# Selective state-space layer on one core: how B and C reach the partitions, how many decay tiles there are, and how the states are summed

## The chip, the cores and the metric

The kernel runs on 1 core of one Trainium2 chip. The metric is device time in microseconds (us), median of the runs. Engines are named as in the profile: PE is TensorE (matmuls; PEld its weight loads), DVE is VectorE, ACT is ScalarE, POOL is GpSimd, SP is SyncE, which here only issues DMAs. SBUF is the working memory of 128 partitions, PSUM a smaller memory of 8 banks per partition (a bank holds 512 float32 columns), into which PE writes.

## The reference

Four layers follow each other on x of shape (16, 256, 256): 16 sequences of T = 256 steps and 256 features. Layer 0 is a low-rank adapter, layer 1 a block with two selective state-space models (one over the sequence, one over the sequence reversed) and an MLP, layers 2 and 3 are attention blocks with MLPs. All is float32. The part that matters here is the state-space model of layer 1, with 512 inner channels and 64 states for each:

```python
xz = h @ in_w
xs, z = jnp.split(xz, 2, axis=-1)
xs = jax.nn.silu(xs)
proj = xs @ xproj_w
dt = jax.nn.softplus(proj[..., :D_INNER] + dt_bias)
Bm = proj[..., D_INNER:D_INNER + D_STATE]
Cm = proj[..., D_INNER + D_STATE:]
A = -jnp.exp(A_log)

def step(hst, ins):
    dt_t, B_t, C_t, x_t = ins
    dA = jnp.exp(dt_t[:, :, None] * A)
    hst = hst * dA + (dt_t * x_t)[:, :, None] * B_t[:, None, :]
    y_t = jnp.einsum('bds,bs->bd', hst, C_t)
    return (hst, y_t)
_, ys = jax.lax.scan(step, h0, (tm(dt), tm(Bm), tm(Cm), tm(xs)))
y = jnp.swapaxes(ys, 0, 1) + xs * Dskip
return y * jax.nn.silu(z) @ out_w
...
h_fwd = _ssm(h, fwd_in_w, ...)
h_bwd = jnp.flip(_ssm(jnp.flip(h, 1), bwd_in_w, ...), 1)
x = x + gate * (h_fwd + h_bwd)
```

## The kernel before

Channels lie on partitions, time on columns. The 512 inner channels are IC = 4 chunks of 128, so a tile of all channels of one sequence is 128 x 4 x 256, or 128x1024. A unit is one sequence in one direction; there are 32. Each unit has NS = 64 states, so the main loop (lines 1145 to 1180) takes 2048 steps k, one state s of one unit u each. For a state:

- `drive` (913), called four steps ahead (AHEAD = 4): POOL multiplies dt*x by this state's row of B and makes h (line 931). The row of B is on all partitions in `bb`, which SP loads for four states at a time by a DMA that reads a row of DRAM once for every partition (`load_b`, 898).
- `decay` (935), called one step ahead: ACT makes exp(dt * A), one instruction a chunk of 128 channels (line 946), into PSUM. The tile holds two chunks, one bank; there are ND = 3 such tiles, used in turn, so a state takes two of them. Column 0 of each chunk is set to 0 once (line 270) and never written again: it ends one chunk's recurrence before the next begins.
- `scan` (965): DVE runs the recurrence over 512 columns at a time, two instructions a state, in place in h (line 974). For the reversed direction the scan reads and writes its columns backwards. Then h is multiplied by the state's row of C. For five states in eight ("near": s % 8 in 0, 2, 3, 5, 6) DVE does it (977), with C in the PSUM tile `cs`, to which PE copies it with two transposes (`spread`, 955); for the other three ("far") POOL does it (981), with C in `cb`, which a DMA loads for the three of eight states (`load_c`, 904).
- `add_up` (984), called two steps later (BEHIND = 2): PE adds h to y in PSUM (line 992), with h as the stationary operand, in eight transposes of 128x128. y therefore has time on partitions. At a unit's end it is copied to SBUF (1165), transposed back (1172) and multiplied with the gate z (1173).

Beside the loop, a few instructions a step, run generators: `beside` (the end of the last unit, `back`, and the projections of the next but one, `front`) and `other` (`rest`: the MLP of layer 1 and layers 2 and 3 of a sequence that is through the state-space part). They share ACT, DVE and PE with the loop; attention adds reductions to DVE (577, 682) and exponentials and copies to ACT. After the last unit the rest of the last sequence runs alone, with the loop's PSUM banks (`alone`).

The order of the instructions on each engine is fixed when the program is built: a scheduler arranges them by what it holds to be ready, and at run time each engine takes them strictly in that order. Only the instructions under `keep_in_program_order` (most of POOL's) stay as written. Between engines, semaphores carry the dependencies: a decay tile is written again only when its last reader on DVE is done, an h buffer (tag h, NH = 11 of them) only when PE has added it.

Of the kernel before, what the change touches and what calls it, by code (L numbers as in the profile page):

```python
# [15 lines left out]
P = 128  # L16
# [5 lines left out]
IC = DI // P  # L22
NS = 64
EPS = 1e-5


COLUMNS = [
# [27 lines left out]
def kernel(ctx: ExitStack, tc: tile.TileContext, a: dict, out: bass.AP):  # L55
# [66 lines left out]


    SG = 4
    ND = 3
    NH = 11
    res = ctx.enter_context(tc.tile_pool(name="res", bufs=1))
    xp = ctx.enter_context(tc.tile_pool(name="xp", bufs=3))
    ws = ctx.enter_context(tc.tile_pool(name="ws", bufs=2))
# [5 lines left out]
    ps_c = ctx.enter_context(tc.tile_pool(name="ps_c", bufs=1, space=PSUM))  # L135
    ps_g = ctx.enter_context(tc.tile_pool(name="ps_g", bufs=2, space=PSUM))

    def chunked(w):
# [234 lines left out]
    def front(u):  # L373
# [27 lines left out]
        yield  # L401
# [5 lines left out]
        bd = bdram.tile([P, T], F32, name="bd")  # L407
        nc.sync.dma_start(bd, bc)
        yield
        pt = bank1("pct")  # L410
        for t in range(NT):
            nc.tensor.transpose(pt[:, t * P : (t + 1) * P], bc[:, t * P : (t + 1) * P], ident)
        cT = s2.tile([P, NT, NS], F32, name="cT")
        nc.scalar.copy(cT, pt[:, :T].rearrange("p (t s) -> p t s", t=NT)[:, :, NS:])
        yield


        pr = s1.tile([P, IC, T], F32, name="pr")
        for m in range(0, IC, 2):
# [42 lines left out]
        st[u] = (xz, cT, bd, dt, dtx)  # L462
        yield

    def back(u, yg):

        b, d = units[u]
        st.pop(u)
        yield
        po = halves(bank1("po"))  # L470
        for m in range(DC):
            for c in range(IC):
                nc.tensor.matmul(
                    po[:, m], w_out[d][:, c, m * P : (m + 1) * P], yg[:, c],
                    start=(c == 0), stop=(c == IC - 1),
                )
            yield
        for m in range(DC):
            xb = xs[b][:, m]
            nc.vector.scalar_tensor_tensor(  # L480
                xb, po[:, m], m_mamba[:, 4 + m, b : b + 1], xb, ALU.mult, ALU.add
            )
        if d == 1:
            waiting.append(rest(b))
        yield
# [404 lines left out]
            yield from front(following)  # L890


    bbs, cbs, ys, made, hs, skips = {}, {}, {}, {}, {}, {}
    cs = ps_c.tile([P, 2, T], F32, name="cs")
    steps = [(u, s) for u in range(len(units)) for s in range(NS)]
    turn = [0]

    def load_b(u, g):
        bd = st[u][2]
        bb = s3.tile([P, SG, T], F32, name="bb")  # L900
        nc.sync.dma_start(bb, bd[g * SG : (g + 1) * SG, :].partition_broadcast(P))
        bbs[u, g] = bb

    def load_c(u, g):
        bd = st[u][2]
        cb = s3.tile([P, 3, T], F32, name="cb")
        nc.sync.dma_start(
            cb,
            bd[NS + 8 * g + 1 : NS + 8 * g + 8 : 3, :].partition_broadcast(P),
        )  # L910
        cbs[u, g] = cb

    def drive(k):
        u, s = steps[k]
        if s % SG == 0:
            if s == 0:
                load_b(u, 0)
            if s + SG < NS:
                load_b(u, s // SG + 1)
            if s % 8 == 0:  # L920
                load_c(u, s // 8)
# [6 lines left out]
        h = s3.tile([P, IC, T], F32, name="h", bufs=NH)  # L928
        bb = bbs[u, s // SG][:, s % SG]
        tc.keep_in_program_order(  # L930
            nc.gpsimd.tensor_tensor(h, st[u][4], bb.unsqueeze(1).to_broadcast([P, IC, T]), ALU.mult)  # L931
        )
        hs[k] = h

    def decay(k):
        u, s = steps[k]
        d = units[u][1]

        when = slice(1, T) if d == 0 else slice(T - 2, None, -1)
        made[k] = []  # L940
        for i in range(2):
            dc = decays[turn[0] % ND]
            turn[0] += 1
            for j in range(2):
                c = 2 * i + (j if d == 0 else 1 - j)
                nc.scalar.activation(  # L946
                    dc[:, j, 1:T], st[u][3][:, c, when], AF.Exp, scale=a_neg[d][:, c, s : s + 1]
                )
            made[k].append(dc)


    near = [k for k, (u, s) in enumerate(steps) if s % 8 in (0, 2, 3, 5, 6)]
    nth = {k: i for i, k in enumerate(near)}

    def spread(i):

        if i >= len(near):
            return
        u, s = steps[near[i]]
        for t in range(NT):  # L960
            nc.tensor.transpose(  # L961
                cs[:, i % 2, t * P : (t + 1) * P], st[u][1][:, t, s : s + 1].to_broadcast([P, P]), ident
            )

    def scan(k):
        u, s = steps[k]
        d = units[u][1]
        h = hs[k]
        for i, dc in enumerate(made.pop(k)):
            hv = h[:, 2 * i : 2 * i + 2].rearrange("p c t -> p (c t)")  # L970
            dv = dc.rearrange("p c t -> p (c t)")
            if d == 1:
                hv = hv[:, ::-1]
            nc.vector.tensor_tensor_scan(hv, dv, hv, 0.0, ALU.mult, ALU.add)  # L974
        if k in nth:
            c = cs[:, nth[k] % 2]
            nc.vector.tensor_tensor(h, h, c.unsqueeze(1).to_broadcast([P, IC, T]), ALU.mult)  # L977
        else:
            c = cbs[u, s // 8][:, (s % 8) // 3]
            tc.keep_in_program_order(  # L980
                nc.gpsimd.tensor_tensor(h, h, c.unsqueeze(1).to_broadcast([P, IC, T]), ALU.mult)  # L981
            )

    def add_up(k):
        u, s = steps[k]
        if s == 0:
            ys[u] = ps_y.tile([P, NT, DI], F32, name="y")

        for n, h in enumerate(([skips.pop(u)] if s == 0 else []) + [hs.pop(k)]):
            for t in range(NT):  # L990
                for c in range(IC):
                    nc.tensor.matmul(  # L992
                        ys[u][:, t, c * P : (c + 1) * P], h[:, c, t * P : (t + 1) * P], ident,
                        start=(s == 0 and n == 0 and c == 0),
                        stop=(s == NS - 1 and c == IC - 1), is_transpose=True,
                        skip_group_check=True,
                    )

# [140 lines left out]
    for k in range(AHEAD):  # L1139
        drive(k)  # L1140
    decay(0)
    spread(0)
    spread(1)
    other = late()
    for k in range(len(steps) + BEHIND):
        if k < len(steps):
# [7 lines left out]
                decay(k + 1)  # L1154
        if k >= BEHIND:
            add_up(k - BEHIND)
        if k - 1 in nth:
            spread(nth[k - 1] + 2)
        if k >= BEHIND:
            u, s = steps[k - BEHIND]  # L1160
            if s == NS - 1:
                b, d = units[u]
                yt = s1.tile([P, NT, DI], F32, name="yt", tag="uu")
                for t in range(NT):
                    nc.scalar.copy(yt[:, t], ys[u][:, t])
                yg = s1.tile([P, IC, T], F32, name="yg", tag="pr")
                for i in range(2):
                    py = halves(bank1("py"))
                    for j in range(2):
                        c = 2 * i + j  # L1170
                        for t in range(NT):
                            nc.tensor.transpose(py[:, j, t * P : (t + 1) * P], yt[:, t, c * P : (c + 1) * P], ident)
                    nc.vector.tensor_tensor(
                        yg[:, 2 * i : 2 * i + 2], py, st[u][0][:, IC + 2 * i : IC + 2 * i + 2], ALU.mult
                    )
                pend = beside((u, yg), u + 2)
        step(pend)
        for _ in range(2 if k % 2 else 1):
# [1 line left out]
                other = waiting.pop(0) if waiting else None  # L1180
    drain(pend)
    drain(other)
    alone += [None] + [t.rearrange("p c t -> p (c t)") for t in (decays[0], cs, decays[1])]
    alone += [None, decays[2].rearrange("p c t -> p (c t)")]
    while waiting:
        drain(waiting.pop(0))

# [27 lines left out]
```

## Time and profile before

The three runs took 7622.63 us (median; 7620.03 to 7626.16).

| | |
|---|---|
| span of the profiled execution | 7616.3 us |
| first scan to last scan | 151 us to 7396 us |
| ACT, 8192 decays (line 946) | 1824.6 + 1816.8 us busy |
| POOL, 2048 products with B (931) | 4793.5 us busy |
| POOL, 768 products with C (981) | 1813.2 us busy |
| PE, 16384 sums (992) | 2385.3 us busy |
| PE, 2560 copies of C (961) | 521.6 us busy |
| DMA, share of 16 engines | 26.7% |

Busy time of an engine is the time in which at least one of its instructions ran. A group's line gives, after the bar, busy time, mean nanoseconds of one instruction, then the engine's idle time just before the group's instructions and what ended most of it. PE's instructions are pipelined, so the mean of one is more than the distance between two. The table of waits gives who waited for whom: total us, how often, the longest.

### The profile page before, as it was taken

The numbers are of one execution on the slowest core, as the hardware profiler recorded it, in microseconds if no ns is written. First come the engines' busy times: TensorE is split into PE (matmuls) and PEld (weight loads), VectorE is DVE, ScalarE is ACT, GpSimd is POOL, SyncE is SP. The second block draws the span as 40 slices with busy tenths as digits, with TensorE's granted clock in tenths as the row PEclk, the third lists the DMA queues.
The fourth block names the chain that finished last, engine by engine and source line by source line (L and its number), as shares of the span: only waits on it lengthen the run. The fifth ranks groups of instructions, "written<-read, shape, count | busy, mean of one in ns | idle before, by whom it ended". The sixth has DMA issues, their size and how long they took to land.

```text
span 7616.3 us, 100847 instructions
## 1 busy us (share of the span) xinstructions
PE 6249.2 (82%) x35471; PEld 4952.4 (65%) x35471; DVE 6860.6 (90%) x6887; ACT 5431.2 (71%) x12141; POOL 6843.8 (90%) x2959
## 2 busy tenths in 40 slices
PE   7568888888888888888888888888888888888778
PEld 4456676666667666676666666666666766666655
DVE  3988999999999999999999999999999999999982
ACT  4567777777777777777777777777777777777753
POOL 3999999999999999999999999999999999999960
PEclk8679999999999999999999999999999999999999
DMA  4112232222322222232222223222232222322221
GB/s 166 54 65 92 89 102 76 87 92 88 103 85 93 80 91 95 92 103 73 88 92 91 100 86 98 78 92 93 87 106 79 94 84 89 101 91 89 73 68 49
DMA packets 331644, 675.90 MB, mean 89 GB/s; under 512 B 24724, under 2 KB 204032, under 8 KB 326784
## 3 DMA queue, kind: packets, MB, share of 16 engines
q1 hardware_dynamic: 331136, 669.44, 26.7%
q8 instruction: 280, 4.59, 0.2%
q14 instruction: 228, 1.87, 0.1%
HBM read 650.22 MB, written 10.75 MB: 87 GB/s over the span
## 4 chain that ended last, share of the span: by engine, by line
DVE 47%; POOL 15%; issue 14%; ACT 12%; PE 10%; DVEq 0%; POOLq 0%; ACTq 0%
DVE h L974 34%; POOL h L931 8%; DVE h L977 8%; ACT decay L946 5%; POOL h L981 5%; PE y L992 3%; DVE maxima L682 1%; ACT L155 1%; PE dense L500 1%; PE down L511 1%; PE bank L108 1%; PE po L605 1%; POOL uu L452 1%; POOL dt L458 1%; POOL dtx L461 1%
## 5 line engine op out<-in xcount | busy, mean ns | idle before, releaser
L974 DVE TENSOR_TENSOR_SCAN h<-decay,h 128x512 f32<-128x512 f32 x4096 | 4748.8, 1213 | 283.1 <-ACT decay L946 196.6
L931 POOL TENSOR_TENSOR h<-dtx,bb 128x1024 f32<-128x1024 f32 x2048 | 4793.5, 2367 | 129.2 <-PE y L992 128.4
L992 PE MATMUL y<-ident,h 128*128 128x128 f32 x16384 | 2385.3, 292 | 693.0 <-POOL h L981 639.1
L992 PEld LDWEIGHTS y<-ident,h 128*128 128x128 f32 x16384 | 2054.6, 151 | 1047.6 <-POOL h L981 733.1
L946 ACT ACTIVATE decay<-dt,a_neg_bwd 128x255 f32<-128x255 f32 x4096 | 1816.8, 471 | 759.9 <-DVE h L974 718.3
L946 ACT ACTIVATE decay<-dt,a_neg_fwd 128x255 f32<-128x255 f32 x4096 | 1824.6, 474 | 613.0 <-DVE h L974 571.6
L981 POOL TENSOR_TENSOR h<-h,cb 128x1024 f32<-128x1024 f32 x768 | 1813.2, 2361 | 289.8 <-DVE h L974 275.1
L977 DVE TENSOR_TENSOR h<-h,cs 128x1024 f32<-128x1024 f32 x1280 | 1533.5, 1215 | 66.2 <-PE cs L961 56.6
L961 PE MATMUL cs<-ident,cT 128*128 128x128 f32 x2560 | 521.6, 294 | 131.8 <-DVE h L977 130.3
L961 PEld LDWEIGHTS cs<-ident,cT 128*128 128x128 f32 x2560 | 331.4, 147 | 216.0 <-DVE h L977 192.0
L572 PE MATMUL sc<-k,q 64*128 64x256 f32 x960 | 293.4, 429 | 16.7 <-ACT ex L581 16.0
L393 PE MATMUL pxz<-hTm,w_in 128*128 128x256 f32 x1024 | 267.6, 388 | 15.9 <-DVE maxima L682 12.1
L679 PE MATMUL sc<-kd,qk 128*128 128x512 f32 x490 | 251.4, 614 | 33.5 <-DVE maxima L682 20.8
L700 PE MATMUL scT<-qk,kd 128*128 128x256 f32 x984 | 251.1, 386 | 28.7 <-DVE qk L691 23.2
L581 ACT ACTIVATE ex<-sc,nmax 128x256 f32<-128x256 f32 x480 | 222.7, 468 | 71.2 <-DVE nmax L577 68.5
L423 PE MATMUL pdt<-xz,w_dt 128*128 128x256 f32 x1024 | 247.3, 385 | 0.0
L572 PEld LDWEIGHTS sc<-k,q 64*128 64x128 f32 x960 | 172.6, 200 | 105.3 <-issue 34.2
L393 PEld LDWEIGHTS pxz<-hTm,w_in 128*128 128x128 f32 x1024 | 181.4, 194 | 53.1 <-DVE maxima L682 15.5
L700 PEld LDWEIGHTS scT<-qk,kd 128*128 128x128 f32 x984 | 175.5, 190 | 60.7 <-ACT pr L429 25.0
L577 DVE TENSOR_REDUCE nmax<-sc 128x2 f32<-128x512 f32 x240 | 163.9, 683 | 49.5 <-PE sc L572 48.8
L423 PEld LDWEIGHTS pdt<-xz,w_dt 128*128 128x128 f32 x1024 | 190.7, 194 | 22.2
L595 ACT COPY exT<-pt 128x512 f32<-128x512 f32 x240 | 140.0, 583 | 86.2 <-PE pt L591 84.0
(350 smaller groups left out, 7571.4 us busy)
## 6 DMA issues: line engine op xcount, KB each, us to landing
bb<-bd SPq DMA_DIRECT2D x512, 512.0 KB
cb<-bd SPq DMA_DIRECT2D x256, 384.0 KB
l2w<-in_L_cond_W_dram SPq DMA_DIRECT2D x32, 1024.0 KB
l3w<-in_L_cond_W_dram SPq DMA_DIRECT2D x32, 1024.0 KB
l1w<-in_L_cond_mlp_w_dram SPq DMA_DIRECT2D x48, 512.0 KB
w_in<-in_L_cond_fwd_in_w_dram SPq DMA_DIRECT2D x16, 1024.0 KB
w_dt<-_L_cond_fwd_xproj_w_dram SPq DMA_DIRECT2D x16, 1024.0 KB
w_in<-in_L_cond_bwd_in_w_dram SPq DMA_DIRECT2D x16, 1024.0 KB
```

What stands on the lines that cost most here:

```text
L393: nc.tensor.matmul(px[:, j], w_in[:, c, (m + j) * P : (m + j + 1) * P], hT[:, c], start=(c == 0), stop=(c == DC - 1),)
L423: nc.tensor.matmul(pp[:, j], w_dt[:, c, (m + j) * P : (m + j + 1) * P], xz[:, c], start=(c == 0), stop=(c == IC - 1),)
L572: nc.tensor.matmul(sc[:, t], q[base : base + 64, ch, t * P : (t + 1) * P], k[base : base + 64, ch], start=True, stop=True,)
L679: nc.tensor.matmul(sc, q[:, g, t * P : (t + 1) * P], kd[g % 2][:, 2 * i : 2 * i + 2], start=True, stop=True)
L700: nc.tensor.matmul(sc[:, kt], kd[g % 2][:, j, kt * P : (kt + 1) * P], q[:, g], start=True, stop=True)
L931: nc.gpsimd.tensor_tensor(h, st[u][4], bb.unsqueeze(1).to_broadcast([P, IC, T]), ALU.mult)
L946: nc.scalar.activation(dc[:, j, 1:T], st[u][3][:, c, when], AF.Exp, scale=a_neg[d][:, c, s : s + 1])
L961: nc.tensor.transpose(cs[:, i % 2, t * P : (t + 1) * P], st[u][1][:, t, s : s + 1].to_broadcast([P, P]), ident)
L974: nc.vector.tensor_tensor_scan(hv, dv, hv, 0.0, ALU.mult, ALU.add)
L977: nc.vector.tensor_tensor(h, h, c.unsqueeze(1).to_broadcast([P, IC, T]), ALU.mult)
L981: nc.gpsimd.tensor_tensor(h, h, c.unsqueeze(1).to_broadcast([P, IC, T]), ALU.mult)
L992: nc.tensor.matmul(ys[u][:, t, c * P : (c + 1) * P], h[:, c, t * P : (t + 1) * P], ident, start=(s == 0 and n == 0 and c == 0), stop=(s == ...
```

## The change

- C: every state's row of C now comes by DMA, four states at a time (`load_c` is like `load_b`); the PE copies, the tile `cs` and the transposed `cT` go. Both kinds of state read C from `cb`.
- Decays: ND = 2 tiles, each of two PSUM banks, 1024 columns, a whole state. Column 0 of a chunk is no longer fixed: dt's column 0 is set to 1e34 (`APART`) by POOL once dt*x has been made, and A is kept at or below -1e-30 (`LEAST`), so the decay there is exp(-1e4 or less) = 0.
- Scan: one instruction of 1024 columns a state. For near states it writes into the decay tile in PSUM, and the multiply by C reads that tile and writes h; for far states it writes h as before.
- Reversed direction: the columns are turned once, when xz is copied out of PSUM, and turned back when `back` reads `po`; the scans run forward for both.
- Sums: PE keeps the identity as the stationary operand and h moves, two matmuls of 512 columns a state. y then has channels on partitions, and the end of a unit is one product with z.
- NH goes from 11 to 10; the list `alone` holds the four halves of the two decay tiles.

```diff
-    ND = 3
-    NH = 11
+    ND = 2
+    NH = 10
...
-        nc.vector.tensor_scalar(an, an, -1.0, None, ALU.mult)
+        nc.vector.tensor_scalar(an, an, -1.0, LEAST, ALU.mult, ALU.min)
...
-    decays = [ps_y.tile([P, 2, T], F32, name=f"decay{j}") for j in range(ND)]
-    for dc in decays:
-        nc.vector.memset(dc[:, :, 0:1], 0.0)
+    decays = [ps_y.tile([P, IC, T], F32, name=f"decay{j}") for j in range(ND)]
...
-            nc.scalar.copy(xz[:, m : m + 2], px)
+            nc.scalar.copy(xz[:, m : m + 2], px[:, :, ::-1] if d else px)
...
+        tc.keep_in_program_order(nc.gpsimd.memset(dt[:, :, 0:1], APART))
...
-                xb, po[:, m], m_mamba[:, 4 + m, b : b + 1], xb, ALU.mult, ALU.add
+                xb, po[:, m, ::-1] if d else po[:, m], m_mamba[:, 4 + m, b : b + 1], xb, ALU.mult, ALU.add
...
     def load_c(u, g):
-        bd = st[u][2]
-        cb = s3.tile([P, 3, T], F32, name="cb")
-        nc.sync.dma_start(
-            cb,
-            bd[NS + 8 * g + 1 : NS + 8 * g + 8 : 3, :].partition_broadcast(P),
-        )
+        bd = st[u][1]
+        cb = s3.tile([P, SG, T], F32, name="cb")
+        nc.sync.dma_start(cb, bd[NS + g * SG : NS + (g + 1) * SG, :].partition_broadcast(P))
...
-        when = slice(1, T) if d == 0 else slice(T - 2, None, -1)
-        made[k] = []
-        for i in range(2):
-            dc = decays[turn[0] % ND]
-            turn[0] += 1
-            for j in range(2):
-                c = 2 * i + (j if d == 0 else 1 - j)
-                nc.scalar.activation(
-                    dc[:, j, 1:T], st[u][3][:, c, when], AF.Exp, scale=a_neg[d][:, c, s : s + 1]
-                )
-            made[k].append(dc)
+        dc = decays[k % ND]
+        for c in range(IC):
+            nc.scalar.activation(dc[:, c], st[u][2][:, c], AF.Exp, scale=a_neg[d][:, c, s : s + 1])
...
     def scan(k):
...
-            nc.vector.tensor_tensor_scan(hv, dv, hv, 0.0, ALU.mult, ALU.add)
-        if k in nth:
-            c = cs[:, nth[k] % 2]
-            nc.vector.tensor_tensor(h, h, c.unsqueeze(1).to_broadcast([P, IC, T]), ALU.mult)
+        h, dc = hs[k], decays[k % ND]
+        c = cbs[u, s // SG][:, s % SG].unsqueeze(1).to_broadcast([P, IC, T])
+        if s % 8 in (0, 2, 3, 5, 6):
+            nc.vector.tensor_tensor_scan(flat(dc), flat(dc), flat(h), 0.0, ALU.mult, ALU.add)
+            nc.vector.tensor_tensor(h, dc, c, ALU.mult)
         else:
...
+            nc.vector.tensor_tensor_scan(flat(h), flat(dc), flat(h), 0.0, ALU.mult, ALU.add)
+            tc.keep_in_program_order(nc.gpsimd.tensor_tensor(h, h, c, ALU.mult))
...
     def add_up(k):
...
-            for t in range(NT):
-                for c in range(IC):
-                    nc.tensor.matmul(
-                        ys[u][:, t, c * P : (c + 1) * P], h[:, c, t * P : (t + 1) * P], ident,
-                        start=(s == 0 and n == 0 and c == 0),
-                        stop=(s == NS - 1 and c == IC - 1), is_transpose=True,
-                        skip_group_check=True,
-                    )
+            for i in range(0, IC, 2):
+                nc.tensor.matmul(
+                    ys[u][:, i : i + 2], ident, h[:, i : i + 2],
+                    start=(s == 0 and n == 0), stop=(s == NS - 1),
+                )
...
-                yt = s1.tile([P, NT, DI], F32, name="yt", tag="uu")
-                for t in range(NT):
-                    nc.scalar.copy(yt[:, t], ys[u][:, t])
                 yg = s1.tile([P, IC, T], F32, name="yg", tag="pr")
-                for i in range(2):
-                    py = halves(bank1("py"))
...
+                nc.vector.tensor_tensor(yg, ys[u], st[u][0][:, IC:], ALU.mult)
```

More of the change, by code (lines that the diff above doesn't have):

```diff
@@ L24 @@
 EPS = 1e-5
+APART, LEAST = 1e34, -1e-30
 COLUMNS = [
@@ L134 @@
     ps_y = ctx.enter_context(tc.tile_pool(name="ps_y", bufs=1, space=PSUM))
-    ps_c = ctx.enter_context(tc.tile_pool(name="ps_c", bufs=1, space=PSUM))
     ps_g = ctx.enter_context(tc.tile_pool(name="ps_g", bufs=2, space=PSUM))
@@ L408, in front @@
         nc.sync.dma_start(bd, bc)
-        yield
-        pt = bank1("pct")
-        for t in range(NT):
-            nc.tensor.transpose(pt[:, t * P : (t + 1) * P], bc[:, t * P : (t + 1) * P], ident)
-        cT = s2.tile([P, NT, NS], F32, name="cT")
-        nc.scalar.copy(cT, pt[:, :T].rearrange("p (t s) -> p t s", t=NT)[:, :, NS:])
         yield
@@ L461, in front @@
         tc.keep_in_program_order(nc.gpsimd.tensor_tensor(dtx, dt, xz[:, 0:IC], ALU.mult))
-        st[u] = (xz, cT, bd, dt, dtx)
+        tc.keep_in_program_order(nc.gpsimd.memset(dt[:, :, 0:1], APART))
+        st[u] = (xz, bd, dt, dtx)
         yield
@@ L890, in beside @@
             yield from front(following)
-    bbs, cbs, ys, made, hs, skips = {}, {}, {}, {}, {}, {}
-    cs = ps_c.tile([P, 2, T], F32, name="cs")
+    bbs, cbs, ys, hs, skips = {}, {}, {}, {}, {}
     steps = [(u, s) for u in range(len(units)) for s in range(NS)]
-    turn = [0]
     def load_b(u, g):
-        bd = st[u][2]
+        bd = st[u][1]
         bb = s3.tile([P, SG, T], F32, name="bb")
@@ L904, in load_c @@
     def load_c(u, g):
-        bd = st[u][2]
-        cb = s3.tile([P, 3, T], F32, name="cb")
-        nc.sync.dma_start(
-            cb,
-            bd[NS + 8 * g + 1 : NS + 8 * g + 8 : 3, :].partition_broadcast(P),
-        )
+        bd = st[u][1]
+        cb = s3.tile([P, SG, T], F32, name="cb")
+        nc.sync.dma_start(cb, bd[NS + g * SG : NS + (g + 1) * SG, :].partition_broadcast(P))
         cbs[u, g] = cb
@@ L919, in drive @@
                 load_b(u, s // SG + 1)
-            if s % 8 == 0:
-                load_c(u, s // 8)
+            load_c(u, s // SG)
         if s == 0:
@@ L930, in drive @@
         tc.keep_in_program_order(
-            nc.gpsimd.tensor_tensor(h, st[u][4], bb.unsqueeze(1).to_broadcast([P, IC, T]), ALU.mult)
+            nc.gpsimd.tensor_tensor(h, st[u][3], bb.unsqueeze(1).to_broadcast([P, IC, T]), ALU.mult)
         )
@@ L937, in decay, with flat @@
         d = units[u][1]
-        when = slice(1, T) if d == 0 else slice(T - 2, None, -1)
-        made[k] = []
-        for i in range(2):
-            dc = decays[turn[0] % ND]
-            turn[0] += 1
-            for j in range(2):
-                c = 2 * i + (j if d == 0 else 1 - j)
-                nc.scalar.activation(
-                    dc[:, j, 1:T], st[u][3][:, c, when], AF.Exp, scale=a_neg[d][:, c, s : s + 1]
-                )
-            made[k].append(dc)
[L952 to L959, printed above, removed]
-        for t in range(NT):
-            nc.tensor.transpose(
-                cs[:, i % 2, t * P : (t + 1) * P], st[u][1][:, t, s : s + 1].to_broadcast([P, P]), ident
-            )
+        dc = decays[k % ND]
+        for c in range(IC):
+            nc.scalar.activation(dc[:, c], st[u][2][:, c], AF.Exp, scale=a_neg[d][:, c, s : s + 1])
+    def flat(t):
+        return t.rearrange("p c t -> p (c t)")
     def scan(k):
         u, s = steps[k]
[L967 to L974, printed above, removed]
-        if k in nth:
-            c = cs[:, nth[k] % 2]
-            nc.vector.tensor_tensor(h, h, c.unsqueeze(1).to_broadcast([P, IC, T]), ALU.mult)
-        else:
[L979 to L982, printed above, removed]
+        h, dc = hs[k], decays[k % ND]
[3 more added lines that the diff above has]
+            nc.vector.tensor_tensor(h, dc, c, ALU.mult)
+        else:
+            nc.vector.tensor_tensor_scan(flat(h), flat(dc), flat(h), 0.0, ALU.mult, ALU.add)
+            tc.keep_in_program_order(nc.gpsimd.tensor_tensor(h, h, c, ALU.mult))
     def add_up(k):
@@ L986, in add_up @@
         if s == 0:
-            ys[u] = ps_y.tile([P, NT, DI], F32, name="y")
+            ys[u] = ps_y.tile([P, IC, T], F32, name="y")
         for n, h in enumerate(([skips.pop(u)] if s == 0 else []) + [hs.pop(k)]):
-            for t in range(NT):
-                for c in range(IC):
-                    nc.tensor.matmul(
-                        ys[u][:, t, c * P : (c + 1) * P], h[:, c, t * P : (t + 1) * P], ident,
-                        start=(s == 0 and n == 0 and c == 0),
-                        stop=(s == NS - 1 and c == IC - 1), is_transpose=True,
-                        skip_group_check=True,
-                    )
+            for i in range(0, IC, 2):
[3 more added lines that the diff above has]
+                )
     turned = [p1.tile([P, DC, B, RANK], F32, name=f"up{k}") for k in range(2)]
@@ L1141 @@
     decay(0)
-    spread(0)
-    spread(1)
     other = late()
@@ L1156 @@
             add_up(k - BEHIND)
-        if k - 1 in nth:
-            spread(nth[k - 1] + 2)
         if k >= BEHIND:
@@ L1162 @@
                 b, d = units[u]
-                yt = s1.tile([P, NT, DI], F32, name="yt", tag="uu")
-                for t in range(NT):
-                    nc.scalar.copy(yt[:, t], ys[u][:, t])
                 yg = s1.tile([P, IC, T], F32, name="yg", tag="pr")
-                for i in range(2):
-                    py = halves(bank1("py"))
[L1169 to L1175, printed above, removed]
+                nc.vector.tensor_tensor(yg, ys[u], st[u][0][:, IC:], ALU.mult)
                 pend = beside((u, yg), u + 2)
@@ L1182 @@
     drain(other)
-    alone += [None] + [t.rearrange("p c t -> p (c t)") for t in (decays[0], cs, decays[1])]
-    alone += [None, decays[2].rearrange("p c t -> p (c t)")]
+    for dc in decays:
+        alone += [None] + [flat(dc[:, i : i + 2]) for i in (0, 2)]
     while waiting:
```

## The prediction, made before the changed kernel was run

> **What bounds the kernel now.** I read the busy line first, then the stretch in which the state loop runs, then the waits of the two fullest engines, then single instructions in time.
>
> ```profile
> PE 6249.2 (82%) x35471; PEld 4952.4 (65%) x35471; DVE 6860.6 (90%) x6887; ACT 5431.2 (71%) x12141; POOL 6843.8 (90%) x2959
> ...
> DVE 47%; POOL 15%; issue 14%; ACT 12%; PE 10%; DVEq 0%; POOLq 0%; ACTq 0%
> ...
> L974 DVE TENSOR_TENSOR_SCAN h<-decay,h 128x512 f32<-128x512 f32 x4096 | 4748.8, 1213 | 283.1 <-ACT decay L946 196.6
> L931 POOL TENSOR_TENSOR h<-dtx,bb 128x1024 f32<-128x1024 f32 x2048 | 4793.5, 2367 | 129.2 <-PE y L992 128.4
> ...
> L946 ACT ACTIVATE decay<-dt,a_neg_bwd 128x255 f32<-128x255 f32 x4096 | 1816.8, 471 | 759.9 <-DVE h L974 718.3
> L946 ACT ACTIVATE decay<-dt,a_neg_fwd 128x255 f32<-128x255 f32 x4096 | 1824.6, 474 | 613.0 <-DVE h L974 571.6
> ...
> L977 DVE TENSOR_TENSOR h<-h,cs 128x1024 f32<-128x1024 f32 x1280 | 1533.5, 1215 | 66.2 <-PE cs L961 56.6
> ```
>
> Two engines are at 90%: DVE and POOL. DVE has the largest part of the chain that ended last, and most of DVE is line 974, the scans. ACT is not full, and before its decays it mostly sits waiting for DVE, that is, for a tile to come free.
>
> The loop runs from 151 us (first scan) to 7396 us (last scan); the rest of the span is 151 us of head and 220 us of tail.
>
> ```profile
> 151.00:7396.00 7245.00, 5959.44 (x34254) 4757.30 (x34255) 6772.02 (x6738) 5298.62 (x11881) 6816.84 (x2935) 0.93 0.27 88
> ```
>
> The columns are the stretch, its length, busy time of PE, PEld, DVE, ACT, POOL, then clock, DMA share, GB/s. DVE: 6772 busy, 473 idle. POOL: 6817 busy, 428 idle. So neither can lose more than 430 to 470 us of waiting, and each is the other's floor.
>
> ```profile
> DVE h L974 <- ACT decay L946: 196.6, 199, 3.2
> DVE h L974 <- POOL h L931: 80.7, 50, 5.9
> DVE h L977 <- PE cs L961: 56.6, 57, 3.5
> DVE nmax L577 <- PE sc L572: 48.8, 32, 3.4
> DVE hT L115 <- ACT bank L113: 39.0, 15, 3.3
> ```
>
> These five are most of DVE's idle time (us in total, times, longest). The largest is the wait for decays, and it is the one that the change touches most.
>
> ```profile
> 3014.29 3.44 DVE L974 TENSOR_TENSOR_SCAN h<-decay,h 128x512 f32<-128x512 f32 x3
> 3017.65 1.20 DVE L977 TENSOR_TENSOR h<-h,cs 128x1024 f32<-128x1024 f32 x1
> 3018.76 0.69 DVE L577 TENSOR_REDUCE nmax<-sc 128x2 f32<-128x512 f32 x1
> 3019.36 3.44 DVE L974 TENSOR_TENSOR_SCAN h<-decay,h 128x512 f32<-128x512 f32 x3
> 3022.91 1.22 DVE L977 TENSOR_TENSOR h<-h,cs 128x1024 f32<-128x1024 f32 x1
> ...
> 3047.66 1.67 ACT L946 ACTIVATE decay<-dt,a_neg_fwd 128x255 f32<-128x255 f32 x4 [0.64 <-DVE h L974]
> ```
>
> Three prices come from here. Scans overlap by 0.10 us: three take 3.44, so one starts (3.44 - 1.21) / 2 = 1.115 after the other. The multiply at 3017.65 starts 0.08 before the scans in front of it have ended (3017.73). The one at 3022.91 follows its own state's scan, must wait for it, and starts 0.11 after its end (3022.80): 0.19 more. Four decays take 1.67, one starting (1.67 - 0.47) / 3 = 0.40 after the other.
>
> **The merged scan.** The 128x512 multiply of line 103 takes 683 ns, the 128x1024 one of 977 1215: 532 ns for 512 columns. A scan of 512 takes 1213 = 2 x 532 + 149, so one of 1024 should take 2 x 1064 + 149 = 2277 and start its successor 2.18 later, against 2 x 1.115 = 2.23. 2048 x -0.05 = -100 us. For the 1280 "near" states the scan now writes PSUM; no wide DVE row does. The nearest: ACT writes 256 columns from PSUM to PSUM in 352 ns (line 113) and from PSUM to SBUF in 458 (552). So -0.1 to +0.1 us each, -130 to +130 in all; I take 0.
>
> **The multiply behind its own scan.** In the order in which the instructions stand on DVE, the multiply of a near state stands directly behind its own last scan in 122 places before and in 922 after, since the whole state is now one scan and no second half stands between. 800 x 0.19 = +152 us. Bounds: 0 to 160.
> The Trainium skill ("VectorE: DVE Perf Modes", The DRAIN you can't avoid) says that a semaphore between chained Vector instructions costs nothing extra, as the pipe empties after each anyway. The two multiplies above differ by 0.19 us; by the rule this term would be 0 and the sum 152 us lower. The row decides.
>
> **C by DMA, no PE copies.** 2560 transposes on line 961 go (0.11 us each start to start, 280 us of PE), and the DVE wait for cs with them: -57 us. In their place cb grows from 256 loads of 384 KB in rows of 1 KB to 512 of 512 KB in rows of 4 KB. In the trace a 4 KB packet takes 159 ns and a 1 KB one 46 ns: 65536 x 159 - 98304 x 46 = 5.9 ms over 16 engines, some 370 us, so the DMA share goes from 27% to about 32%. One load is 128 x 159 / 16 = 1.3 us of transfer. It is issued on SP when the group before last has been multiplied, four states (about 13 us) ahead of its use, and SP's order also holds weight loads that waited up to 27 us for PE. Cost 0, hidden by those four states; bound above: one load in ten 3 us late, 51 x 3 = 150.
>
> **Sums.** Eight transposes a state (1.04 us in the timeline) become two matmuls of 512 columns; such matmuls (line 773) start 0.43 us apart, so 0.86. PE ends some 300 us emptier, and it does not set the end: 0. The yt copies (64 x 0.58 us of ACT) and the cT copies go, the final product becomes 32 of 1024 columns instead of 64 of 512: within 3 us. Ten h buffers instead of eleven add to POOL's wait for y (128 us now), which counts only while POOL sets the pace. The reversals (one ACT copy, one read of po) and the 32 memsets of four columns: 0.
>
> **Two decay tiles instead of three.** This is the large term. Before, a ring of three half-state tiles: while DVE scans one half, two more can stand ready, and a tile freed now is needed two scans (2.2 us) later; two decays (0.88 us) fill it. After, a ring of two whole-state tiles: the tile freed when state j-1 is done (for a near state after its multiply) must be full one state later (2.2 us for a far state, 3.4 for a near one), and four decays take 1.67. That alone fits. What does not fit is the order on ACT. There, in 531 of the 2048 states, one to three decays of state j+1 stand ahead of the last decay of state j. The first of them waits for DVE to finish j-1; DVE, done with j-1, needs j, whose last decay is behind it. So DVE goes idle for a round trip that no lead of ACT can hide: 0.03 from DVE's end to ACT's start (the gap of nearly all 1443 waits), 0.40, 0.47, 0.03 to 0.10 back, about 0.95 to 1.0 with one decay in between, up to 2.3 with more. In 318 of the states no other DVE work stands in the gap; in the rest a reduction (0.6) or the like does. Sum over the 531: 580 us. Before, the same crossing is harmless, because a filled third tile lies between.
> The shorter lead also uncovers long ACT pieces: a table load, a 2048-wide silu and a second load are 1.28 + 1.92 + 1.28 = 4.5 us. Adding, along DVE's order, every stretch "a tile comes free, ACT works up to the decay that DVE needs" that is longer than DVE's work meanwhile (stretches that don't overlap, ACT at these rows, 0.2 us for the handovers and the lost overlap) gives 910 us in 650 places after, and 133 us in 134 places before, where the trace has 197 + 199 x 0.1 = 217. ACT's own waits for PE are not in these sums; I add the missing 84 to both: 990 after, +773. Bounds: the crossings alone, with what there was (580); and the whole sum scaled by 217 / 133 (1480, +1260).
>
> **What goes in return.** With DVE that much slower POOL (6817 busy) is always ahead: of the 81 us of waits for its h, -70. Of the waits for sc and hT (88 us): between 0 and -88, I take -40.
>
> Sum: -100 + 152 - 57 + 773 - 70 - 40 = +658 us. The loop goes to 7903, the span from 7616.3 to 8274. The median of the runs shown (7622.63) lies 6 us above that span, so 8280.
>
> **Rivals.** (1) The detours vanish and the change gains. POOL, not DVE, would set the pace and DVE's lead (h is made four states ahead) would swallow them. For it: POOL is as full as DVE, and POOL's waits for line 974 are only 275 us. Against: DVE's steps and its idle time fill the loop exactly, and a round trip cannot be prepared. Then -100 + 152 - 57 - 70 - 40 = -115: 7510. It decides where the decay waits grow by less than 115 us, that is 0.18 us for each of the 650 places. (2) Only the crossings cost, the long ACT pieces fall into other waits: +580 - 115 = +465: 8090. (3) ACT's waits for PE (135 us at q, 84 at exT, 86 at the norm) pass through the shorter ring: +1260 - 115: 8770. (4) C comes late, nothing of the decays: 150 - 115, about 7660: POOL and DVE both would wait on DMA, of which the trace of before shows no case at bb.
>
> **Numbers.** Forecast 0.60, (1) 0.06, (2) 0.20, (3) 0.11, (4) 0.03. The forecast's own range is 8130 to 8430 (PSUM writes, and DMA on top). To hold 8 in 10 it reaches below (2), whose lower half would need the gaps half covered, and halfway to (3): 7950 to 8600. What a measurement here can tell from no change is about 0.2% (15 us). Faster: 0.06; within it 0.02; slower 0.92.
>
> **What would show it.** DVE's scans waiting for ACT decays: 850 to 1100 us in 600 or more waits, many near 0.9 us; POOL's waits for DVE several times 275; a scan of 1024 columns at about 2.28; multiplies starting 0.1 after their scan's end; no wait for cb. If the decay waits stay under 400 us, the ring argument is wrong; if DVE waits for DMA, the C term is.

## The result, and the profile after

The changed kernel takes 8930.78 us (median of four runs, 8930.06 to 8932.46) against 7624.4 us of the kernel before beside it: 1.171 times as long, 95% interval 1.1693 to 1.1726, or 1306 us more. The forecast was 8280 (7950 to 8600): the direction was right, the size was half.

The first view is the page of the changed kernel: busy time, share of the span and instructions of each engine, then the state loop's groups. After a group's bar stand busy time, mean ns of one, the idle time before it and what ended most of it.

```profile
PE 7590.2 (85%) x24271; PEld 4228.4 (47%) x24271; DVE 6920.2 (78%) x4804; ACT 5585.5 (63%) x12045; POOL 6843.0 (77%) x2991
...
L918 POOL TENSOR_TENSOR h<-dtx,bb 128x1024 f32<-128x1024 f32 x2048 | 4796.7, 2356 | 1653.0 <-PE y L950 1563.9
L950 PE MATMUL y<-h,ident 128*128 128x512 f32 x8192 | 4014.3, 621 | 128.4 <-POOL h L941 121.0
L937 DVE TENSOR_TENSOR_SCAN decay<-decay,h 128x1024 f32<-128x1024 f32 x1280 | 2934.9, 2294 | 1081.7 <-POOL h L918 535.6
...
L940 DVE TENSOR_TENSOR_SCAN h<-decay,h 128x1024 f32<-128x1024 f32 x768 | 1753.3, 2283 | 360.1 <-POOL h L918 280.1
L941 POOL TENSOR_TENSOR h<-h,cb 128x1024 f32<-128x1024 f32 x768 | 1808.5, 2355 | 43.2 <-issue 28.4
L938 DVE TENSOR_TENSOR h<-decay,cb 128x1024 f32<-128x1024 f32 x1280 | 1560.1, 1222 | 67.9 <-DVE decay L937 1.8
```

DVE and POOL do the work they did before (6920 and 6843 us) and have fallen from 90% to 78 and 77% of the span. PE was to lose 300 us; it has gained 7590 - 6249 = 1341. Line 950 tells why by its count: `add_up` issues two matmuls a state, 4096 in all, and the trace has 8192. Each float32 matmul of 512 columns is two instructions on PE. POOL, which had waited 128 us for PE's y, waits 1564.

The second view is the table of waits: total us, how often, the longest.

```profile
POOL h L918 <- PE y L950: 1563.9, 724, 8.9
...
DVE decay L937 <- POOL h L918: 535.6, 290, 4.2
DVE decay L937 <- ACT decay L927: 319.8, 286, 3.0
DVE h L940 <- POOL h L918: 280.1, 165, 6.6
...
PE y L950 <- DVE yg L1116: 254.9, 31, 10.5
```

The chain runs from PE through the h buffers: PE adds a state late, its buffer comes free late, POOL makes the next h late, DVE waits 816 us for it (81 before). DVE's waits for decays, the centre of the forecast, are 319.8 plus 79.7 for line 940, about 400 instead of 850 to 1100.

The third view is PE's timeline: start, length, instruction, count.

```profile
3015.51 1.88 PE L950 MATMUL y<-h,ident 128*128 128x512 f32 x4
3017.23 1.89 PE L504 MATMUL down<-q,l2out 128*128 128x256 f32 x8
3018.96 1.88 PE L950 MATMUL y<-h,ident 128*128 128x512 f32 x4
```

One state's sum is a block of four. From its start to the start of the next instruction it holds PE for 3017.23 - 3015.51 = 1.72 us, 0.43 an instruction. A block of eight transposes in the kernel before:

```profile
3019.51 1.04 PE L992 MATMUL y<-ident,h 128*128 128x128 f32 x8
3020.48 1.09 PE L605 MATMUL po<-exT,v 128*64 128x256 f32 x8
```

Its length is 1.04 us, against 1.88 for the four; it holds PE for 3020.48 - 3019.51 = 0.97. Over the whole trace such transposes start 0.109 us apart (median), eight of them 0.87. So a state's sum now takes PE about twice as long.

### The profile page after: what moved, and what is told of

Same layout as the page of the kernel before. It is cut to its first block, busy times and chain, and to the rows that moved or that the text cites. A ratio compares the mean times of both kernels' runs of the same rounds, so it can differ in the third digit from the quotient of the medians.

```text
span 8929.0 us, 76800 instructions
## 1 busy us (share of the span) xinstructions
PE 7590.2 (85%) x24271; PEld 4228.4 (47%) x24271; DVE 6920.2 (78%) x4804; ACT 5585.5 (63%) x12045; POOL 6843.0 (77%) x2991
## 3 DMA queue, kind: packets, MB, share of 16 engines
q1 hardware_dynamic: 302464, 837.23, 28.1%
## 5 line engine op out<-in xcount | busy, mean ns | idle before, releaser
L950 PE MATMUL y<-h,ident 128*128 128x512 f32 x8192 | 4014.3, 621 | 128.4 <-POOL h L941 121.0
L937 DVE TENSOR_TENSOR_SCAN decay<-decay,h 128x1024 f32<-128x1024 f32 x1280 | 2934.9, 2294 | 1081.7 <-POOL h L918 535.6
L927 ACT ACTIVATE decay<-dt,a_neg_bwd 128x256 f32<-128x256 f32 x4096 | 1891.8, 474 | 1528.4 <-DVE h L938 967.2
L927 ACT ACTIVATE decay<-dt,a_neg_fwd 128x256 f32<-128x256 f32 x4096 | 1905.5, 475 | 1233.0 <-DVE h L938 897.9
L950 PEld LDWEIGHTS y<-h,ident 128*128 128x128 f32 x8192 | 1583.3, 199 | 1682.2 <-issue 1443.8
L940 DVE TENSOR_TENSOR_SCAN h<-decay,h 128x1024 f32<-128x1024 f32 x768 | 1753.3, 2283 | 360.1 <-POOL h L918 280.1
L938 DVE TENSOR_TENSOR h<-decay,cb 128x1024 f32<-128x1024 f32 x1280 | 1560.1, 1222 | 67.9 <-DVE decay L937 1.8
L950 PE MATMUL y<-skip,ident 128*128 128x512 f32 x128 | 111.5, 1024 | 254.9 <-DVE yg L1116 254.9
L110 PE MATMUL bank<-sq,onesm 128*128 128x256 f32 (+1 forms) x312 | 108.5, 480 | 111.8 <-ACT sq L107 111.8
L584 PE MATMUL pt<-ident,ex 128*128 128x128 f32 x960 | 167.1, 300 | 42.8 <-ACT q L602 42.7
```

The lines of the kernel that those rows point to most:

```text
L927: nc.scalar.activation(dc[:, c], st[u][2][:, c], AF.Exp, scale=a_neg[d][:, c, s : s + 1])
L937: nc.vector.tensor_tensor_scan(flat(dc), flat(dc), flat(h), 0.0, ALU.mult, ALU.add)
L938: nc.vector.tensor_tensor(h, dc, c, ALU.mult)
L940: nc.vector.tensor_tensor_scan(flat(h), flat(dc), flat(h), 0.0, ALU.mult, ALU.add)
L950: nc.tensor.matmul(ys[u][:, i : i + 2], ident, h[:, i : i + 2], start=(s == 0 and n == 0), stop=(s == NS - 1),)
```

## The experiments

Two theories stood against each other. A: PE's time in the sums sets the pace. B: the two whole-state decay tiles do. All times are medians, beside the kernel before on the same chip (7623 to 7628 us).

### One part at a time

**Changed kernel, old sums.** `add_up` and the unit's end as before; the rest as changed.

```diff
-                nc.tensor.matmul(ys[u][:, i : i + 2], ident, h[:, i : i + 2], ...)
+                    nc.tensor.matmul(
+                        ys[u][:, t, c * P : (c + 1) * P], h[:, c, t * P : (t + 1) * P], ident,
+                        ..., is_transpose=True, skip_group_check=True,
```

> The changed kernel with one part undone: the sums again by eight transposes a state, and the unit's end turned back as before. Theory A (PE sets the pace: a 512-column float32 matmul is two instructions of 0.43 us, so the sums cost 3.5 ms of PE instead of 1.8): PE busy falls from 7590 to about 5900 us, POOL's wait for y from 1564 to under 300, the time to 7850 to 8250 us. Theory B (the ring of two decay tiles is the cost, as predicted): the time stays above 8700 us.

Measured: 8669.11, ratio 1.1361 (1.1342 to 1.138), 1041 us over the kernel before, between the two expectations. The busy line and the waits of this run:

```profile
PE 6518.1 (75%) x32847; PEld 5030.0 (58%) x32847; DVE 6871.8 (79%) x4836; ACT 5556.2 (64%) x12109; POOL 6833.2 (79%) x2991
...
DVE decay L937 <- ACT decay L927: 660.2, 321, 5.5
...
DVE h L940 <- ACT decay L927: 211.8, 192, 3.8
DVE nmax L570 <- PE sc L565: 139.5, 41, 5.2
DVE hT L117 <- ACT bank L115: 87.8, 31, 4.9
```

With PE out of the way the decay waits are there: 660 + 212 = 872 us, where the forecast had 990. How one of them arises stands in ACT's timeline of this run, in brackets the idle time before:

```profile
2484.02 1.67 ACT L927 ACTIVATE decay<-dt,a_neg_bwd 128x256 f32<-128x256 f32 x4 [0.44 <-DVE h L938]
2485.71 1.28 ACT L358 ACT_TABLE_LOAD   x1
2487.01 0.60 ACT L358 ACTIVATE dtx<-phigh 128x512 f32<-128x512 f32 x1
2487.62 1.28 ACT L156 ACT_TABLE_LOAD   x1
2488.92 0.87 ACT L927 ACTIVATE decay<-dt,a_neg_bwd 128x256 f32<-128x256 f32 x2
...
2489.43 4.48 DVE L937 TENSOR_TENSOR_SCAN decay<-decay,h 128x1024 f32<-128x1024 f32 x2 [5.50 <-ACT decay L927]
```

DVE's next scan starts after 5.50 us of idling: 3.2 us of table loads and their instruction lay between ACT and the last decay that this scan needed. Two of the four decays in front (0.4 us each) belong to a later state, by the order of the built program, so a crossing is part of this wait too.

**Kernel before, new sums.**

```diff
-                    nc.tensor.matmul(ys[u][:, t, ...], h[:, c, t * P : (t + 1) * P], ident, ..., is_transpose=True, ...)
+                nc.tensor.matmul(ys[u][:, i : i + 2], ident, h[:, i : i + 2], ...)
```

> The kernel before with one part of the change alone: the sums with h as the moving operand (and the unit's end that goes with it). Theory A: PE busy rises from 6249 to about 7950 us, and since the PE copies of C are still there the time is 9000 to 9400 us, above the changed kernel's. Theory B: the three decay tiles are still there, so 7600 to 7750 us.

Measured: 8838.73, ratio 1.1585 (1.1567 to 1.1602), +1211. Theory A's side, somewhat less than it asked for. The waits repeat those of the changed kernel, with the old decay tiles and hardly a wait for them:

```profile
POOL h L931 <- PE y L991: 1562.3, 696, 8.6
DVE h L974 <- POOL h L931: 1277.1, 683, 6.9
...
DVE h L974 <- ACT decay L946: 56.4, 95, 2.3
```

So the old sums with the rest of the change lose 1041 us, and the new sums in the kernel before (where PE also still copies C) lose 1211. Both together lose 1306, not 2250: while DVE waits for a late h, ACT fills the decay tiles.

**Half of the sums.** One of the two matmuls of a state left out.

```diff
-            for i in range(0, IC, 2):
+            for i in range(0, IC, 2) if s in (0, NS - 1) else (2 * (s % 2),):
```

> The changed kernel with one of the two 512-column matmuls of the sums left out in each state but the first and the last of a unit (half of the sum is left out; everything that waits for it stays). PE loses about 1950 matmuls of 0.86 us, some 1670 us of its 7590. Theory A (PE's time in the sums paces the changed kernel through the h buffers): POOL's h waits for PE's y fall from 1564 us to under 300, and the time comes down to what the decay tiles alone cost, 8500 to 8720 (the run with transposed sums has 8669). Rival (not PE's time, but the order of the sums and y's two banks at a unit's end): above 8850.

Measured: 8743.67, ratio 1.1471 (1.1451 to 1.1491), 24 us above the range of theory A. POOL's h line has lost its wait entirely, and DVE's decay waits are back:

```profile
L918 POOL TENSOR_TENSOR h<-dtx,bb 128x1024 f32<-128x1024 f32 x2048 | 4769.0, 2356 | 0.3 <-PE y L950 0.2
```

```profile
DVE decay L937 <- ACT decay L927: 698.2, 396, 7.3
DVE h L940 <- ACT decay L927: 322.6, 260, 4.3
```

Only matmuls of PE are left out (the order in which the scheduler puts the other instructions changes with them), and the limit moved from PE to the tiles.

### The order of the decays

Decays on ACT and scans on DVE were each held in the order of the states, so that no decay of a later state stands ahead of one of an earlier.

```diff
+            after_last("ACT",
                 nc.scalar.activation(dc[:, c], st[u][2][:, c], AF.Exp, scale=a_neg[d][:, c, s : s + 1])
+            )
...
+            after_last("DVE", nc.vector.tensor_tensor_scan(...))
```

> The changed kernel with its decays on ACT and its scans on DVE pinned to the order of the states, so that no decay of state j+1 stands ahead of one of state j (576 states before, 0 now). Theory A: within 1.5% of the changed kernel, 8800 to 9000 us, since PE is the one that is late. Theory B: the round trips go, 8350 to 8550 us.

> Both edits: sums by transposes, decays and scans pinned to the order of the states. It shows what the crossed decays cost once PE is not late. If they cost what the prediction said (about 1 us each), this is 300 to 450 us below the run with transposed sums alone (435 crossed states there); if waits elsewhere hide them, within 60 us of it.

Measured: 8816.17, ratio 1.1554 (1.1537 to 1.1571), 115 us below the changed kernel, as theory A has it. With the old sums 8419.98, ratio 1.1036 (1.102 to 1.1053): 249 us below the 8669, between the two expectations (within 60, 300 to 450). There DVE's decay waits are 682 us still:

```profile
DVE decay L950 <- ACT decay L939: 433.8, 220, 8.3
DVE h L953 <- ACT decay L939: 248.0, 104, 9.8
```

The order is worth some 250 us of theory B's loss, where the forecast had 580 for the crossings. It is not the crossings alone: in the built program of the run with the old sums 694 states are crossed in the order in which DVE takes them (the expectation says 435), and in 510 places DVE takes a state before the one ahead of it; holding the order undoes both. The same edit on the kernel before:

> The kernel before, with decays on ACT and scans on DVE each held in the order of the states (as in the two runs in order). With a filled third tile between, crossings were harmless before by the prediction: 7560 to 7640, at best some of the 197 us of decay waits. If crossings cost before too: under 7530.

Measured: 7597.44, ratio 0.9968 (0.9956 to 0.998): 26 us faster than the kernel before, the only version here that beats it. Its decay waits are not lower (259 against 197 us); what fell are POOL's waits for y (128 to 59) and DVE's for h (81 to 17).

### Cutting the dependence

ACT writes its decays to a spare tile that nobody reads.

```diff
+    for dc in decays:
+        nc.vector.memset(dc, 0.0)
+    aside = res.tile([P, T], F32, name="aside")
...
-            nc.scalar.activation(dc[:, c], st[u][2][:, c], ...)
+            nc.scalar.activation(aside, st[u][2][:, c], ...)
```

> The changed kernel with the sums of before, and ACT's decays written to a spare SBUF tile that nobody reads; the scans run on tiles that are set once (so the recurrence is not the reference's). Every instruction of ACT, DVE, POOL and PE stays, only the dependence between decays and scans is gone. Theory B (the 1041 us that the changed kernel with the sums of before loses come from the two whole-state tiles, directly or through what they push late): 7350 to 7650. Rival R (the rest of the change, the far multiply order, C by DMA or PE's lower clock, costs a part by itself): above 7900.

> The kernel before with the same cut (decays to a spare SBUF tile, scans on tiles set once) and ten h buffers, for the room. It prices the ring of three half-state tiles: both theories expect about the 200 us of DVE's decay waits less, 7400 to 7500. If it is far lower, the ring before cost more than its waits show.

> The changed kernel itself, with the same cut. Theory A (PE's time in the sums sets the pace whatever the decays do): 8600 to 8850, as the run of the kernel before with moving sums (8839), POOL's waits for PE's y still over 1200 us. If the decay tiles are the larger part after all: below 8200.

Measured: 8409.38, ratio 1.1033 (1.1018 to 1.1048); the kernel before 7897.06, ratio 1.0359 (1.0345 to 1.0374); the changed kernel 9054.3, ratio 1.1879 (1.1863 to 1.1895). The second spoils the test: without its decay dependence the kernel before got slower by 273 us. Two things changed beside the dependence. The scheduler arranges an engine by what it holds to be ready, so with the dependence gone it built another order, and other things came late. And the spare tile lies in SBUF, where a decay takes 507 ns instead of 471 to 474, so that ACT is busy 5858 us in this run instead of 5431. Which of the two costs the 273 us was not separated. The waits of the first:

```profile
POOL h L921 <- PE y L954: 669.7, 145, 18.7
...
POOL uu L447 <- ACT uu L442: 396.9, 14, 38.9
```

In the run with the old sums these two were 0.2 and 37.7 us. So 8409 doesn't settle what the tiles cost. The third, with the same two side effects, is above its range, but one thing holds in it: with no decay to wait for at all, the new sums make POOL wait 1614 us for y.

### Half-state tiles, and a collision

To give theory B its own test, the same four PSUM banks were cut into four half-state tiles, with the scan and the multiply in place in h. Two more runs vary it: three such tiles, and the whole-state tiles with the near scan writing h.

```diff
-        dc = decays[k % ND]
+            dc = decays[(2 * k + c // 2) % ND]
...
-            nc.vector.tensor_tensor_scan(flat(dc), flat(dc), flat(h), 0.0, ALU.mult, ALU.add)
-            nc.vector.tensor_tensor(h, dc, c, ALU.mult)
+            nc.vector.tensor_tensor_scan(hv, flat(dc), hv, 0.0, ALU.mult, ALU.add)
+            nc.vector.tensor_tensor(h, h, c, ALU.mult)
```

> The changed kernel with the sums of before and four decay tiles of one PSUM bank each (the same PSUM as two of two banks), two scans of 512 columns a state in place in h, the multiply by C in place in h; C by DMA, reversal at xz, decay at column 0 from dt as changed. Theory B (of the 1041 us that the changed kernel with the sums of before loses, all is the ring of whole-state tiles): decay waits of DVE under 200 us, time 7500 to 7720. Rival R (C by DMA, its larger transfers or its SBUF reads, cost a part): above 7900 with decay waits just as low.

> As the run with four half-state tiles, but with three, as many as before the change: what is left of the change is C by DMA, the reversal, ten h buffers and column 0. Theory B: decay waits about the 197 us of before, no wait for cs, time 7570 to 7720. Rival R: as far above 7630 as the run with four tiles, or further.

> The changed kernel with the sums of before, and the near states' scan writing h instead of the decay tile, the multiply reading h: the whole-state tile comes free one multiply (1.2 us) earlier in 1280 of 2048 states. Theory B: the detours through ACT get shorter for near states, decay waits from 872 us to 500 to 700, time 8350 to 8520. Rival R (not the ring): within 50 us of 8669.

Measured: 8956.4, ratio 1.1743 (1.1725 to 1.176); 8984.35, ratio 1.1781 (1.1763 to 1.1798); 9556.87, ratio 1.2535 (1.2504 to 1.2566). By the letter the first two are for rival R. The third fits neither: its decay waits fell from 872 to 562 us, as theory B has it, and its time rose by 888. The groups of the run with three tiles show a cause that neither theory had:

```profile
L918 POOL TENSOR_TENSOR h<-dtx,bb 128x1024 f32<-128x1024 f32 x2048 | 5715.4, 2813 | 160.9 <-PE y L952 160.9
...
L940 DVE TENSOR_TENSOR h<-h,cb 128x1024 f32<-128x1024 f32 x1280 | 2674.0, 2089 | 13.6
```

The multiply now has both inputs in SBUF and takes 2089 ns instead of 1215; POOL's product beside it takes 2813 instead of 2367. Both engines are at 88 to 89% of a longer span, doing the same work slower. The experiment had put a new cost beside the one it was to measure, so it was made again.

### Half-state tiles, with the multiply reading PSUM

Near scans stay in place in the half tiles, and two multiplies of 512 columns read them there.

```diff
+        for i in range(2):
+            out = flat(dv[i] if near else hv[i])
+            nc.vector.tensor_tensor_scan(out, flat(dv[i]), flat(hv[i]), 0.0, ALU.mult, ALU.add)
+        if near:
+            for i in range(2):
+                nc.vector.tensor_tensor(hv[i], dv[i], c.to_broadcast([P, 2, T]), ALU.mult)
```

> The changed kernel with the sums of before and four decay tiles of one PSUM bank; two scans of 512 columns a state, for near states in place in the decay tiles, then two multiplies of 512 columns that read them from PSUM (no multiply reads two SBUF operands, as it does in the earlier run with four half tiles). The multiplies cost 1280 x (2 x 0.68 - 1.22) = 180 us more on DVE. Theory B (the 1041 us of the run with transposed sums come from the whole-state grain of the ring): decay waits under 400 us and 7700 to 8000. Rival R (C by DMA, the reversal or the low clock cost about 400 by themselves): 8150 or more.

> The same with three half-state tiles, as before the change. Theory B (the number of tiles matters little next to their grain, and a near half now holds its tile until its multiply): 100 to 400 us over the run with four. Rival R: within 50 us of it.

> Four half-state tiles as in the first run of this group, with decays on ACT and scans on DVE held in the order of the states. Theory B: what crossings are left go, 100 to 250 us below the first run. Rival R: within 50 us of it.

Measured: four tiles 7866.45, ratio 1.0321 (1.0305 to 1.0336); three 8218.6, ratio 1.0781 (1.0763 to 1.0799); four in order 7870.38, ratio 1.0323 (1.0308 to 1.0339). The run with four:

```profile
PE 6192.5 (79%) x32847; PEld 4813.4 (61%) x32847; DVE 6970.7 (89%) x8164; ACT 5405.6 (69%) x12109; POOL 6839.4 (87%) x2991
```

```profile
DVE decay L941 <- ACT decay L927: 169.6, 138, 4.5
...
DVE h L941 <- ACT decay L927: 38.4, 28, 2.8
```

The same four banks, in halves, take 8669 - 7866 = 803 us off, though DVE is busy 6970.7 - 6871.8 = 99 us longer with two multiplies for one; decay waits are 208 us, about what they were before the change. C by DMA, the reversal, column 0 and ten h buffers are in this run, which is 244 us over the kernel before, 110 of them (6970.7 - 6860.6) more work on DVE; so they are not where the 1041 went, though how much of the other 134 is theirs was not separated. The order of the decays no longer matters here (4 us, for rival R), although 542 states are still crossed in the built program; that an early decay now finds a free tile would explain it. With both in order, halves against whole tiles are worth 8419.98 - 7870.38 = 550 us; the rest of the 803 is the order that comes with whole tiles.

Three half tiles are 352 us slower than four, as theory B has it. They are also 596 us slower than the kernel before, which has three of the same size, and DVE's decay waits are 550 us against 197. A near half is now held until its multiply is done, and before only until its scan was: the time for which a tile is held counts as well as the number of tiles. That this is the whole of the 596 was not shown.

The ring alone, with nothing else changed, is the kernel before with two half-state tiles in use:

```diff
-    ND = 3
+    ND = 2
```

> The kernel before with two half-state decay tiles instead of three, and nothing else: the ring alone, made shorter. Theory B: a tile freed by a scan must be full one scan (1.2 us) later, and two decays with their handovers take 0.95 to 1.0, so each piece of other ACT work between shows: over 8300, with decay waits over 700 us. Rival R (lead on ACT is not what counts): under 7900.

Measured: 8154.29, ratio 1.0697 (1.0681 to 1.0713), +531, between the two expectations, below theory B's 8300 but with its waits:

```profile
DVE h L974 <- ACT decay L946: 739.7, 493, 7.5
```

## Why the prediction was right in direction and wrong in size

**Sums: the step that failed.** "Eight transposes a state (1.04 us in the timeline) become two matmuls of 512 columns; such matmuls (line 773) start 0.43 us apart, so 0.86. PE ends some 300 us emptier, and it does not set the end: 0." The 0.43 was right and was multiplied by the wrong count: the row holds instructions, and a matmul in the code is two. Four times 0.43 is 1.72. The 1.04 for the transposes is the length of a block and not what it keeps PE from the next instruction, which is 0.87 to 0.97; by that measure even the forecast's 0.86 would have saved hardly anything. So a state got some 0.8 us dearer on PE, not 0.18 cheaper. The page of before could have told: line 393 issues 512 matmuls and its group counts 1024, while line 992 issues eight transposes for each of 2048 states and counts 16384.

```profile
L992 PE MATMUL y<-ident,h 128*128 128x128 f32 x16384 | 2385.3, 292 | 693.0 <-POOL h L981 639.1
...
L393 PE MATMUL pxz<-hTm,w_in 128*128 128x256 f32 x1024 | 267.6, 388 | 15.9 <-DVE maxima L682 12.1
```

The term that the forecast put at 0 costs 1211 us in the kernel before, and in the changed kernel it sets the pace through POOL's wait for y. In no rival was PE the limit.

The Trainium skill ("FP8 and Floating Point Precision", TensorE Precision Notes) has a float32 matmul go through the array in four passes; the rows here show it as two instructions. "TensorE: Matmul & The Clock Gate" (Terms) calls the transpose mode four times faster for float32. Here eight transposes hold PE for 0.87 to 0.97 us and four instructions for 1.72, for the same 1024 columns, a factor of about two; the direction of that rule speaks against this change, and the forecast had not weighed it.

**Two decay tiles: right mechanism, seen only when PE was taken away.** Forecast 990 us of decay waits, 872 measured with the old sums. In the changed kernel they are 400, since DVE is held up by h first. The forecast had named "under 400" as the sign that the argument was wrong; that sign holds only while DVE sets the pace. The whole forecast, +658 with the sums at 0, is to be held against the 1041 us of the run with the old sums: this term's waits came out lower (675 us more than before, forecast 773), the time higher. The missing part is in the forecast's return of -40 for sc and hT: with the old sums DVE's waits for them rose from 88 to 227 us, those for hd and py from 26 to 102. Halves in the same banks gave back 803 us net, some 900 with the dearer multiplies counted; how that splits between these chains was not separated. The split of the term was off too: crossings were to be 580, and the whole order is worth some 250; long ACT pieces, such as the table loads shown, are among the rest. (The forecast counts 531 crossed states; the built program, like the expectation of the run in order, has 576.)

**Return for POOL's waits: -70 forecast, +735 measured.** "POOL (6817 busy) is always ahead" took the h buffers for granted; with PE late, POOL is behind it. The wait that DVE had for POOL's h went from 81 to 816 us.

**Terms that held.** A scan of 1024 columns takes 2283 to 2294 ns (forecast 2277), and writing it to PSUM adds 11 ns. DVE's busy time is within 60 us of before, so the merged scan did little, as computed. In the run with the old sums a multiply behind its own scan starts 2.32 us after that scan, where another scan starts 2.21 after it: 0.11 lost, forecast 0.19, so some 90 us for the 800 places instead of 152. The DMA share is 28.1% of a longer span (8929 x 0.281 - 7616 x 0.267 = 475 us as a mean over the 16 engines, forecast 370; the forecast's 32% is of the old span, of its own 8274 us it would be 29%), and no wait for cb appears among the waits of the changed kernel, as forecast.

**The rivals.** None came true. The gain (1) would have needed both tiles and sums to be free; (3), at 8770, lay nearest in time, by luck: its cause was another. The direction was no luck, since the tiles alone lose 1041 us, but in the changed kernel it is not they that set the pace. What was missing was a rival in which the engine that was to be relieved becomes the limit.

## What to carry to other kernels

Before costing an operation by a row's distance, divide the row's count by the number that the code issues: a float32 matmul here was two instructions, a transpose one. Count a ring in pieces, and in how long each is held, before its bytes: the same four banks cost some 800 us more as two tiles than as four, 550 of them with the order of the instructions held. When two costs each set the pace, the waits of one hide the other's; undo each part alone before believing a table of waits.

## What the runs showed of the hardware beyond that

A VectorE multiply with both inputs in SBUF and a GpSimd product did not run side by side here. In the run with three half tiles, 1203 of the 1280 multiplies began while a POOL product ran; they end 1.08 us after that product's end (10th to 90th percentile 1.080 to 1.087), which is about a multiply's own time (1.2 us), so they must have waited for it. POOL's products with B fall into two groups, near 2.36 us and near 3.33 us. With one input in PSUM, as in the kernel before and in the changed one, the multiply takes 1.22 us, although 1203 and 1055 of its 1280 began while a POOL product ran. The Trainium skill ("SBUF — State Buffer", Who interferes with whom) describes this as an exclusive lock on a port pair that the two engines share; the 1.08 us agree.

The granted TensorE clock tends to be lower where PE is less dense: 0.963 with the new sums on the kernel before (PE 87% busy), 0.945 in the changed kernel (85%), 0.859 with the old sums (75%), 0.823 in the slowest run (72%). The busy share alone doesn't set it: at 79% it was 0.876 with three half tiles read in PSUM and 0.919 in the kernel before with two. What the clock alone costs was not tried.
